# Unprocessed slots of all batches moved behind one branch at the end, in a state-space and mixture-of-experts kernel

## The chip, the cores and the metric

The kernel runs on one core of one Trainium2 chip. The metric is the device time of one execution in microseconds, as the median of several runs. An execution that is profiled gives in addition a trace of every engine: TensorE (PE), VectorE (DVE), ScalarE (ACT), GpSimd (POOL) and the DMA queues, which SyncE (SP) and POOL feed here.

## The reference

The inputs are x of 4 x 512 x 512 (batch, row, feature) and a context of 4 x 512 x 256, all fp32. Two blocks follow each other, each added to x behind a gate:

```python
x = x + tanh(g_xattn[0]) * ssm(ctx, layernorm(x), in_proj_w, conv_w, ...)   # a scan over 512 positions
x = x + tanh(g_ffn[0]) * moe(layernorm(x), W1, Wg, W2, Ws1, Wsg, Ws2, gate_w, gate_b, biases)
...
def step(state, xs):                      # 512 channels, 16 states each
    state = state * exp(d_t[..., None] * A) + (d_t * u_t)[..., None] * B_t[:, None, :]
    y_t = einsum('ben,bn->be', state, C_t)
...
output = expert(x, Ws1, Wsg, Ws2)         # shared: silu(x @ w1) * (x @ wg) @ w2, all 512 wide
for e in range(7):                        # each row goes to 3 of 7 experts
    output = output + expert(x, W1[e], Wg[e], W2[e]) * w_e[..., None]
```

## The kernel before, in words

The work of one batch has two halves. The first is the scan (`loop`, lines 549 to 725): 32 steps, each one state and 256 of the 512 channels. In a step POOL multiplies the rows B into the inputs (L637), ACT makes the decays `da` (L648), DVE scans (L679), multiplies by C (L595) and adds up (L602). The rows B and C come in groups of two states as `bc` (L324), one transfer of 1 MB on SP's queue for four steps. For batch 0 PE adds up instead of DVE (L609).

The second half is the mixture of experts. `post` turns y, adds it to x, normalizes (L756) and turns the result (`pn`, L764; copied by ACT at L767). `route` computes the logits (`pl` on PE, L820; `lg` on ACT, L822), ranks the experts on DVE, and gives each pair of row and expert a place, so that the rows of one expert stand together in tiles of 128 rows; POOL scatters the rows to their places in the DRAM tensor `xs` (L933, twelve indirect DMAs). `xs` exists twice, and batches take turns. The tensors are cleared at the start by `clear` (L208), three tiles a transfer.

The number of tiles depends on the data: with 512 x 3 pairs and 7 experts it is at most 18 (`n_slot`); 13 (`n_full`) are always processed. `experts` does so: the shared expert first (p1s, p2s, pos), then the tiles 0 to 12, each with its own expert's weights `w` (three transfers of 1 MB, addressed by a register that SP loads from the batch's `table`, L950 and L957), the gathered rows `xt` (L986), two products, their gating on DVE (L1155), a turn, a third product `po`, a scaling on ACT (L1015) and an indirect DMA that adds the rows to the output (L1020, POOL).

Tiles beyond the 13 are `rest` (L1027 to L1046): a branch on the count of tiles, `tc.If(n > i)` at L1029, whose body processes one tile and holds the branch for the next. The count is loaded into a register of all five engines at the last tile (L1215) and `rest` follows the last tile of each batch. At the end of an untaken branch each engine makes up for the semaphore counts of the body, and SP waits for the semaphores of its DMA queues.

The order of the work is written out by hand. Both halves are generators; `moe` runs post, route and experts, and between its pieces the scan of the next batch is moved on by as many steps as the table `STEPS` says (per batch: one digit for each piece of `post`, one for each of `experts`). `PIECES` does the same for what prepares the batch after that (`ahead`). Engines work their instructions off in this order.

Of the kernel before, what the change touches and what calls it, by code (L numbers as in the profile page):

```python
# [10 lines left out]
F32 = mybir.dt.float32  # L11
# [6 lines left out]
P = 128  # L18
# [3 lines left out]
NE = 7  # L22
# [13 lines left out]
STEPS = {  # L36
    0: ("000000", "101011010100110100110120111101110200010101111101101001"),
    1: ("100000", "201001001010110100110201201101110100101101201101100101"),
    2: ("000001", "201011010000110100110200011100200110101110200111000000"),
    3: ("000000", "000000000000000000000000000000000000000000000000000000"),  # L40
}

PIECES = {
    0: "000000002010112021101100222002011020220222010002201110",
    1: "000000101100111111111012112002022101122210211002100001",
    2: "",
# [5 lines left out]
def gated_ssm_moe(  # L52
# [29 lines left out]
    n_slot = lambda nt: (nt * P * TOPK + NE * (P - 1)) // P  # L82
    NSLOT = n_slot(NC)

    const = ctx.enter_context(tc.tile_pool(name="const", bufs=1))
# [56 lines left out]

    between = const.tile([P, 1], F32, tag="between", name="between")
    mhalf = const.tile([P, NC], F32, tag="mhalf", name="mhalf")
    nc.gpsimd.memset(mhalf, -0.5)
# [41 lines left out]

    xs = [store.tile([NSLOT * P, D + NW], F32, tag=f"xs{k}", name=f"xs{k}") for k in range(2)]

# [12 lines left out]
    def clear():  # L202

        nc.sync.dma_start(acc[(B - 1) * L : (B - 1) * L + P, :], empty[0][:, 0:D])
        for dst, src in zip(xs, empty):
            for i in range(0, NSLOT, 3):
                k = min(3, NSLOT - i)
                nc.sync.dma_start(  # L208
                    dst[i * P : (i + k) * P, :].rearrange("(i p) d -> p i d", p=P),
                    src.unsqueeze(1).to_broadcast([P, k, D + NW]),  # L210
                )
                yield
# [518 lines left out]

    held, routed = {}, {}

# [79 lines left out]
    def route(q):  # L813
# [98 lines left out]
        posk = tile_("posk", [nt, TOPK])  # L912
        nc.vector.tensor_reduce(posk, pk, AX.X, ALU.add)
        place = small.tile([P, nt, TOPK], I32, tag="place", name=f"place_{q}")
        nc.vector.tensor_copy(place, posk)
# [9 lines left out]
        nc.vector.tensor_reduce(expert, past, AX.X, ALU.add)  # L925
        table = small.tile([P, slots + 1], I32, tag="table", name=f"table_{q}")
        nc.vector.tensor_scalar(table[:, 0:slots], expert, NE - 1.0, None, ALU.min)
        nc.vector.tensor_copy(table[:, slots : slots + 1], upto[:, NE - 1 : NE])  # L928
        routed[q] = expert, table

        for t in range(nt):
            for k in range(TOPK):
                put = nc.gpsimd.indirect_dma_start(  # L933
                    xs[q % 2], bass.IndirectOffsetOnAxis(ap=place[:, t, k : k + 1], axis=0), xns[:, t, :], None
                )
# [48 lines left out]
    def rows_in(q, i):  # L984
        xt = two.tile([P, D + NW], F32, tag="xt", bufs=4, name=f"xt_{q}_{i}")[:, 0:D]
        nc.sync.dma_start(xt, xs[q % 2][ts(i, P), 0:D])  # L986
        return xt

    def slot_rows(q, expert):
# [4 lines left out]
        ex = small.tile([P, slots, NW], F32, tag="ex", name=f"ex_{q}")  # L994
        nc.sync.dma_start(ex, xs[q % 2][0 : slots * P, D : D + NW].rearrange("(i p) c -> p i c", p=P))
        yield
# [7 lines left out]
        nc.vector.tensor_tensor(of, of, ex[:, :, 0:NE], ALU.mult)  # L1004
        weight = small.tile([P, slots], F32, tag="weight", name=f"weight_{q}")
        nc.vector.tensor_reduce(weight, of, AX.X, ALU.add)
        nc.vector.scalar_tensor_tensor(weight, ex[:, :, NE], b * L - 0.5, weight, ALU.is_gt, ALU.mult)
        row = small.tile([P, slots], I32, tag="row", name=f"row_{q}")
        nc.vector.tensor_copy(row, ex[:, :, NE])
# [14 lines left out]

    slot_of = {}

    def rest(q, i, table, n, into):  # L1027
# [20 lines left out]
    def experts(q):  # L1048
# [144 lines left out]
        for i in range(last_tile + 1):  # L1193
# [19 lines left out]
            if i > 2:  # L1213
                W[i - 1].load(2)
            if i == last_tile:  # L1215
                n = nc.values_load(
                    table[0:1, slots : slots + 1], min_val=0, max_val=slots,
                    skip_runtime_bounds_check_because="no more tiles than slots can be in use",
                )
            yield  # L1220
# [33 lines left out]
            if i == last_tile:  # L1254
                W[i].load(2)

                into = [wpool.tile([P, NC, D], F32, tag=f"w{k}", name=f"w{k}_r{q}") for k in range(3)]
                if q + 1 < len(CHUNKS):
# [28 lines left out]
        else:  # L1287
            while adds:
                adds.pop(0)()
        rest(q, last_tile + 1, table, n, into)  # L1290

    def moe():
# [5 lines left out]
        for q, (b, _, _) in enumerate(CHUNKS):  # L1298
# [6 lines left out]
            for i, _ in enumerate(experts(q)):  # L1305
# [4 lines left out]
                if q + 1 < len(CHUNKS) and CHUNKS[q + 1][0] in loop_done:  # L1310
# [3 lines left out]
                    if more:  # L1314
                        yield q + 1, 0, next(at[q + 1])

    def first_loads():
# [75 lines left out]
```

## Time and profile before

| what | value |
| --- | --- |
| median of 3 runs | 1055.65 us (1055.58 to 1058.12) |
| the profiled execution | 1059.25 us |
| its span from first to last instruction | 1057.2 us |
| mean granted TensorE clock | 0.96 |
| batch 0's first logits to its last tile | 168 to 404 us |
| batch 1's | 412 to 642 us |
| batch 2's | 643 to 851 us |
| batch 3's | 852 to 1046 us |

The page of the profile gives busy times by engine, then the span in 40 slices (each digit a tenth), then what waited for what. An engine's idle time is named by what released it: "PE pn L764 <- PEq L1029" means that PE's instruction of line 764 stood behind an instruction of line 1029 in PE's own queue. Slices of PE, DVE, the granted clock and the DMA engines:

```profile
PE   9587867799999897999999888899999999999995
DVE  6999978999999997899999999888999531100000
PEclk9699888899999998999999999999999999999998
DMA  4197420499899965689899945889999449999974
```

### The profile page before, as it was taken

To read this page: it belongs to the slowest core of one execution; us is meant where nothing else is said; L and a number is where in the kernel's file an instruction comes from. 1 tells how busy PE (TensorE), PEld (TensorE's weight loads), DVE (VectorE), ACT (ScalarE), POOL (GpSimd) and SP (SyncE) were. 2 spreads that over 40 slices of the span, in tenths; PEclk is the share of its full clock that TensorE was granted. 3 is DMA by queue.
4 is the path that set the end of the run, shared out by engine and by line. 5 is a ranking of instruction groups with operands and counts; after the bars stand their busy time and mean duration, and the time that the engine had idled before them with its cause. 6 is when DMAs were issued, how large, how long until landed. Compare 5 with 4: busy or idle time off the path is not lost. (4 is left out here: it accounts for less than half of the span.)

```text
span 1057.2 us, 8951 instructions
## 1 busy us (share of the span) xinstructions
PE 952.6 (90%) x2540; PEld 430.9 (41%) x2540; DVE 798.7 (76%) x987; ACT 551.5 (52%) x770; POOL 497.4 (47%) x328
## 2 busy tenths in 40 slices
PE   9587867799999897999999888899999999999995
PEld 3232323344344443434344443344444444444442
DVE  6999978999999997899999999888999531100000
ACT  5857733547696664446797745536677220122221
POOL 2489942563564643653645546744565214011111
PEclk9699888899999998999999999999999999999998
DMA  4197420499899965689899945889999449999974
GB/s 141 53 345 262 160 80 0 157 332 331 282 355 318 324 186 188 214 322 353 298 331 295 369 122 192 290 281 336 375 376 362 133 146 341 345 318 322 340 233 83
DMA packets 138043, 272.11 MB, mean 257 GB/s; under 512 B 17134, under 2 KB 17134, under 8 KB 137982
## 3 DMA queue, kind: packets, MB, share of 16 engines
q1 hardware_dynamic: 126174, 244.19, 65.5%
q0 software_dynamic: 11328, 26.42, 10.8%
q10 hardware_dynamic: 480, 0.79, 0.2%
q8 instruction: 26, 0.43, 0.2%
q14 instruction: 35, 0.29, 0.1%
HBM read 230.65 MB, written 40.71 MB: 257 GB/s over the span
## 5 line engine op out<-in xcount | busy, mean ns | idle before, releaser
L637 POOL TENSOR_TENSOR h<-bc,home 128x1024 f32<-128x1024 f32 x128 | 309.2, 2422 | 238.6 <-DVE home L602 200.0
L981 PE MATMUL p<-w,turned_x 128*128 128x512 f32 x824 | 374.5, 598 | 12.4 <-ACT h L1238 4.7
L679 DVE TENSOR_TENSOR_SCAN h<-da,h 128x512 f32<-128x512 f32 x256 | 297.5, 1206 | 9.3 <-ACT da L648 6.8
L648 ACT ACTIVATE da<-home,a_neg 128x512 f32<-128x512 f32 x256 | 174.5, 689 | 226.6 <-DVE h L679 225.8
L981 PEld LDWEIGHTS p<-w,turned_x 128*128 128x128 f32 x824 | 152.7, 191 | 188.4 <-issue 168.7
L981 PE MATMUL po<-w,turned_h 128*128 128x512 f32 x408 | 185.4, 598 | 7.7 <-ACT yo L1015 5.1
L1020 POOL DMA_INDIRECT out_dram<-yo,row x52 | 95.9, 1845 | 189.0 <-ACT yo L1015 156.4
L595 DVE TENSOR_TENSOR h<-h,bc 128x1024 f32<-128x1024 f32 x96 | 135.8, 1415 | 1.0
L1155 DVE TENSOR_TENSOR h<-h,p 128x512 f32<-128x512 f32 x51 | 34.2, 671 | 120.0 <-PE p L981 120.0
L602 DVE TENSOR_TENSOR home<-home,h 128x1024 f32<-128x1024 f32 x96 | 119.6, 1246 | 3.1
L981 PEld LDWEIGHTS po<-w,turned_h 128*128 128x128 f32 x408 | 74.2, 192 | 84.6 <-issue 74.7
L609 PE MATMUL sum<-hc,ident 128*128 128x512 f32 x128 | 69.3, 684 | 21.7 <-POOL hc L595 12.1
L933 POOL DMA_INDIRECT xs<-xn,place x48 | 55.6, 1159 | 44.7 <-DVE table L928 25.1
L648 ACT ACT_TABLE_LOAD x53 | 68.0, 1283 | 1.3 <-ACT xd L318 0.4
L973 ACT COPY turned_x<-pt_x 128x512 f32<-128x512 f32 x52 | 30.2, 581 | 67.3 <-PE pt_x L968 67.2
L1015 ACT ACTIVATE yo<-po,weight 128x512 f32<-128x512 f32 x52 | 35.5, 683 | 55.1 <-PE po L981 49.7
L1114 PE MATMUL pos<-w_s,home 128*128 128x512 f32 x128 | 58.4, 610 | 4.0 <-DVE home L1078 2.3
L981 PE MATMUL p1s<-home,w_s 128*128 128x512 f32 x128 | 59.1, 599 | 1.7 <-ACT sgs L1075 1.7
L981 PE MATMUL p2s<-home,w_s 128*128 128x512 f32 x128 | 60.0, 612 | 0.0
L973 ACT COPY turned_h<-pt_h 128x512 f32<-128x512 f32 x51 | 29.5, 578 | 44.2 <-PE pt_h L968 44.2
L609 PEld LDWEIGHTS sum<-hc,ident 128*128 128x128 f32 x128 | 25.6, 212 | 63.4 <-issue 25.7
L1238 ACT ACT_TABLE_LOAD x38 | 48.8, 1283 | 0.5
(160 smaller groups left out, 848.0 us busy)
## 6 DMA issues: line engine op xcount, KB each, us to landing
w<-in_w_dram SPq DMA_DIRECT2D x104, 1024.0 KB, 8.3
w<-in_wg_dram SPq DMA_DIRECT2D x52, 1024.0 KB, 10.8
bc<-rows SPq DMA_DIRECT2D x32, 1024.0 KB, 6.6
xt<-xs SPq DMA_DIRECT2D x52, 256.0 KB, 6.5
xs<-empty SPq DMA_DIRECT2D x12, 780.0 KB, 11.0
w_s<-in_ws_dram SPq DMA_DIRECT2D x8, 1024.0 KB, 9.3
xx<-in_x_dram SPq DMA_DIRECT2D x4, 1024.0 KB, 7.4
w_s<-in_wsg_dram SPq DMA_DIRECT2D x4, 1024.0 KB, 11.4
```

The source lines that it names most:

```text
L595: engine.tensor_tensor(hc, h, c_k.unsqueeze(1).to_broadcast([P, W, L]), ALU.mult)
L602: nc.vector.tensor_tensor(y[:, c0 : c0 + W, :], y[:, c0 : c0 + W, :], h, ALU.add)
L609: nc.tensor.matmul(sums[c1 + w], ident, hc1[:, w, :], start=False, stop=(k1 == NS - 1))
L637: nc.gpsimd.tensor_tensor(h, b_k.unsqueeze(1).to_broadcast([P, W, L]), layer.u[:, c0 : c0 + W, :], ALU.mult)
L648: nc.scalar.activation(da, layer.delta[:, c, :], AF.Exp, scale=a_neg[:, c, k : k + 1])
L679: nc.vector.tensor_tensor_scan(h[:, w, :], da, h[:, w, :], 0.0, ALU.mult, ALU.add)
L933: put = nc.gpsimd.indirect_dma_start(xs[q % 2], bass.IndirectOffsetOnAxis(ap=place[:, t, k : k + 1], axis=0), xns[:, t, :], None)
L973: nc.scalar.copy(t, pt)
L981: nc.tensor.matmul(p[:, 0:n], lhs(c), rhs(c), start=(c == 0), stop=(c == NC - 1))
L1020: nc.gpsimd.indirect_dma_start(acc, bass.IndirectOffsetOnAxis(ap=slot_of[q][1][:, i : i + 1], axis=0), yo, None, compute_op=ALU.add,)
L1114: nc.tensor.matmul(pos[t], hTs[:, c, ts(t, P)], ws.t[2][:, c, :], start=(c == 0), stop=(c == NC - 1))
L1238: nc.scalar.activation(hs[i], p1.pop(i), AF.Silu)
```

## The change

- The call of `rest` at the end of each batch goes, and with it the load of the count at the last tile. A new function `rests`, called once after the last batch, loads the largest count of the four batches (`most`) and holds all four batches' `rest` chains, each with its own count, behind one branch.
- So that the rows beyond 13 tiles outlive their batch, `xs` becomes one tensor: two halves of 13 tiles that batches take turns in, and four stretches of 5 tiles, one for each batch. `clear` fills 46 tiles instead of 36, in 17 transfers instead of 12. Places of 13 x 128 and over are moved by an offset: two more small DVE operations in `route`, and one that keeps the largest count. The weights' rows `ex` come in two transfers instead of one. `table`, `weight` and `row` are kept for all four batches.
- The digits of `STEPS` and `PIECES` are other ones.

```diff
 STEPS = {
-    0: ("000000", "101011010100110100110120111101110200010101111101101001"),
-    1: ("100000", "201001001010110100110201201101110100101101201101100101"),
-    2: ("000001", "201011010000110100110200011100200110101110200111000000"),
+    0: ("000000", "101011010100110100110120111101110200000201102101101000"),
+    1: ("100100", "021001001001101100110201201101110100101101201101100101"),
+    2: ("000001", "110011010020000200101101101101110110110002011101000000"),
...
 PIECES = {
-    0: "000000002010112021101100222002011020220222010002201110",
-    1: "000000101100111111111012112002022101122210211002100001",
+    0: "000000002010111121101100222002011002122210211010120011",
+    1: "000000101100110211021021202002021220222120011102000001",
...
-    xs = [store.tile([NSLOT * P, D + NW], F32, tag=f"xs{k}", name=f"xs{k}") for k in range(2)]
+    xs = store.tile([(2 * NF + B * NR) * P, D + NW], F32, tag="xs", name="xs")
+    first_place = lambda q: q % 2 * NF * P
+    rest_place = lambda q: (2 * NF + q * NR) * P
+    tile_place = lambda q, i: first_place(q) + i * P if i < NF else rest_place(q) + (i - NF) * P
...
-        for dst, src in zip(xs, empty):
-            for i in range(0, NSLOT, 3):
-                k = min(3, NSLOT - i)
+        parts = [(first_place(k), NF, empty[k]) for k in range(2)]
+        parts += [(rest_place(0), (B - 1) * NR, empty[0]), (rest_place(B - 1), NR, empty[1])]
+        for at, n, src in parts:
+            for i in range(0, n, 3):
+                k = min(3, n - i)
...
+        beyond = tile_("beyond", [nt, TOPK])
+        nc.vector.tensor_scalar(
+            beyond, posk, NF * P - 0.5, float(rest_place(q) - NF * P - first_place(q)), ALU.is_gt, ALU.mult
+        )
+        nc.vector.scalar_tensor_tensor(posk, posk, float(first_place(q)), beyond, ALU.add, ALU.add)
...
+        if q == 0:
+            nc.vector.tensor_copy(most, upto[:, NE - 1 : NE])
+        else:
+            nc.vector.tensor_tensor(most, most, upto[:, NE - 1 : NE], ALU.max)
...
+    def rests():
+        slots = n_slot(NC)
+        number = small.tile([P, 1], I32, tag="number", name="number")
+        nc.vector.tensor_copy(number, most)
...
+        n = count_of(number[0:1, 0:1])
+        into = [wpool.tile([P, NC, D], F32, tag=f"w{k}", name=f"w{k}_r") for k in range(3)]
+        with tc.If(n > NF):
+            for q in range(len(CHUNKS)):
+                rest(q, NF, tables[q], count_of(tables[q][0:1, slots : slots + 1]), into)
...
-            if i == last_tile:
-                n = nc.values_load(
-                    table[0:1, slots : slots + 1], min_val=0, max_val=slots,
-                    skip_runtime_bounds_check_because="no more tiles than slots can be in use",
-                )
...
-        rest(q, last_tile + 1, table, n, into)
...
+        rests()
```

More of the change, by code (lines that the diff above doesn't have):

```diff
@@ L83, in gated_ssm_moe @@
     NSLOT = n_slot(NC)
+    NF = n_full(NC)
+    NR = NSLOT - NF
     const = ctx.enter_context(tc.tile_pool(name="const", bufs=1))
@@ L143, in gated_ssm_moe @@
     between = const.tile([P, 1], F32, tag="between", name="between")
+    most = const.tile([P, 1], F32, tag="most", name="most")
     mhalf = const.tile([P, NC], F32, tag="mhalf", name="mhalf")
@@ L204, in clear @@
         nc.sync.dma_start(acc[(B - 1) * L : (B - 1) * L + P, :], empty[0][:, 0:D])
-        for dst, src in zip(xs, empty):
-            for i in range(0, NSLOT, 3):
-                k = min(3, NSLOT - i)
+        parts = [(first_place(k), NF, empty[k]) for k in range(2)]
[3 more added lines that the diff above has]
+                k = min(3, n - i)
                 nc.sync.dma_start(
-                    dst[i * P : (i + k) * P, :].rearrange("(i p) d -> p i d", p=P),
+                    xs[at + i * P : at + (i + k) * P, :].rearrange("(i p) d -> p i d", p=P),
                     src.unsqueeze(1).to_broadcast([P, k, D + NW]),
@@ L729, in ssm @@
             yield from loop(b, sums if b == 0 else None)
-    held, routed = {}, {}
+    held, routed, tables = {}, {}, {}
     def post(q):
@@ L925, in route @@
         nc.vector.tensor_reduce(expert, past, AX.X, ALU.add)
-        table = small.tile([P, slots + 1], I32, tag="table", name=f"table_{q}")
+        table = small.tile([P, slots + 1], I32, tag="table", bufs=B, name=f"table_{q}")
         nc.vector.tensor_scalar(table[:, 0:slots], expert, NE - 1.0, None, ALU.min)
@@ L929, in route @@
         routed[q] = expert, table
+        tables[q] = table
+        if q == 0:
+            nc.vector.tensor_copy(most, upto[:, NE - 1 : NE])
+        else:
+            nc.vector.tensor_tensor(most, most, upto[:, NE - 1 : NE], ALU.max)
         for t in range(nt):
@@ L933, in route @@
                 put = nc.gpsimd.indirect_dma_start(
-                    xs[q % 2], bass.IndirectOffsetOnAxis(ap=place[:, t, k : k + 1], axis=0), xns[:, t, :], None
+                    xs, bass.IndirectOffsetOnAxis(ap=place[:, t, k : k + 1], axis=0), xns[:, t, :], None
                 )
@@ L985, in rows_in @@
         xt = two.tile([P, D + NW], F32, tag="xt", bufs=4, name=f"xt_{q}_{i}")[:, 0:D]
-        nc.sync.dma_start(xt, xs[q % 2][ts(i, P), 0:D])
+        nc.sync.dma_start(xt, xs[tile_place(q, i) : tile_place(q, i) + P, 0:D])
         return xt
@@ L994, in slot_rows @@
         ex = small.tile([P, slots, NW], F32, tag="ex", name=f"ex_{q}")
-        nc.sync.dma_start(ex, xs[q % 2][0 : slots * P, D : D + NW].rearrange("(i p) c -> p i c", p=P))
+        for i, n in ((0, NF), (NF, NR)):
+            at = tile_place(q, i)
+            nc.sync.dma_start(ex[:, i : i + n, :], xs[at : at + n * P, D : D + NW].rearrange("(i p) c -> p i c", p=P))
         yield
@@ L1004, in slot_rows @@
         nc.vector.tensor_tensor(of, of, ex[:, :, 0:NE], ALU.mult)
-        weight = small.tile([P, slots], F32, tag="weight", name=f"weight_{q}")
+        weight = small.tile([P, slots], F32, tag="weight", bufs=B, name=f"weight_{q}")
         nc.vector.tensor_reduce(weight, of, AX.X, ALU.add)
         nc.vector.scalar_tensor_tensor(weight, ex[:, :, NE], b * L - 0.5, weight, ALU.is_gt, ALU.mult)
-        row = small.tile([P, slots], I32, tag="row", name=f"row_{q}")
+        row = small.tile([P, slots], I32, tag="row", bufs=B, name=f"row_{q}")
         nc.vector.tensor_copy(row, ex[:, :, NE])
@@ L1025, in gated_ssm_moe, with count_of @@
     slot_of = {}
+    def rests():
+        slots = n_slot(NC)
+        number = small.tile([P, 1], I32, tag="number", name="number")
+        nc.vector.tensor_copy(number, most)
+        def count_of(ap):
+            return nc.values_load(
+                ap, min_val=0, max_val=slots,
+                skip_runtime_bounds_check_because="no more tiles than slots can be in use",
+            )
+        n = count_of(number[0:1, 0:1])
[3 more added lines that the diff above has]
+                rest(q, NF, tables[q], count_of(tables[q][0:1, slots : slots + 1]), into)
     def rest(q, i, table, n, into):
@@ L1255, in experts @@
                 W[i].load(2)
-                into = [wpool.tile([P, NC, D], F32, tag=f"w{k}", name=f"w{k}_r{q}") for k in range(3)]
                 if q + 1 < len(CHUNKS):
```

## The prediction, made before the result was known

> **What bounds the kernel now.** I read the page's busy list and slices first, then the busy time by stage, then the branch's line, then the timeline around it, and last the chain that ended last.
>
> ```profile
> span 1057.2 us, 8951 instructions
> PE 952.6 (90%) x2540; PEld 430.9 (41%) x2540; DVE 798.7 (76%) x987; ACT 551.5 (52%) x770; POOL 497.4 (47%) x328
> ...
> xt<-xs SPq DMA_DIRECT2D x52, 256.0 KB, 6.5
> ```
>
> PE is busy for 90%, but no engine bounds all stages. 52 gathered tiles are read, 4 batches of 13, so with these inputs no batch has a 14th tile: the branch is never taken, before or after. All that is at stake is what an untaken branch, its place and the order cost. Busy time by stage (columns: PE, PEld, DVE, ACT, POOL, granted clock, DMA):
>
> ```profile
> 225.00:400.00 175.00, 167.29 (x465) 76.79 (x463) 172.56 (x186) 117.40 (x162) 88.72 (x41) 0.98 0.90 301
> 400.00:460.00 60.00, 53.38 (x135) 22.88 (x135) 50.76 (x80) 27.11 (x36) 36.89 (x35) 0.94 0.64 212
> 460.00:640.00 180.00, 168.26 (x480) 78.18 (x479) 176.17 (x194) 122.47 (x169) 88.47 (x43) 0.99 0.89 300
> 640.00:700.00 60.00, 51.72 (x123) 21.22 (x122) 50.04 (x78) 27.80 (x35) 39.76 (x35) 0.97 0.69 225
> 700.00:850.00 150.00, 148.03 (x441) 71.70 (x440) 129.15 (x136) 89.58 (x121) 71.69 (x35) 1.00 0.93 317
> 850.00:1034.00 184.00, 182.45 (x505) 84.73 (x504) 22.44 (x64) 35.07 (x58) 31.66 (x36) 1.00 0.88 289
> ```
>
> During the tiles of batches 0 and 1 (225 to 400, 460 to 640) DVE, which runs the scan of the next batch, is busy for 98.6 and 97.9%: it sets the pace. From about 700 on PE does (98.7%, then 99.2%). Between them lie two passages of 60 us, each the start of a batch, in which neither is full: PE lacks 6.6 and 8.3 us, DVE 9.2 and 10.0. A gain must come from there, from 850, or from the tail. Now the branch's own line, and who waited for it:
>
> ```profile
> L1029 SPq EVENT_SEMAPHORE  x36: 17/17/17, 400.5 to 1039.9; - x36
> L1029 SPq COMPARE_BRANCH  x4: 45/48/50, 400.0 to 1034.0; - x4
> ...
> L1029 PEldq COMPARE_BRANCH  x4: 424/1680/6429, 400.8 to 1042.9; - x4
> L1029 ACTq COMPARE_BRANCH  x4: 45/45/45, 404.5 to 1046.0; - x4
> ...
> L1029 POOLq COMPARE_BRANCH  x4: 53/53/53, 405.0 to 1046.7; - x4
> ...
>   PE pn L764: 3.1, 1
>   PE pl L820: 0.9, 1
> ```
>
> The branch stands four times, once a batch. It takes 45 to 72 ns on every engine but PE, where it takes up to 6.4 us. The timeline from 407 shows what followed the 6.4 us one:
>
> ```profile
> 407.51 2.50 PE L764 MATMUL pn<-ident,xn 128*128 128x128 f32 x16 [3.06 <-PEq L1029]
> ...
> 411.62 5.54 PE L820 MATMUL pl<-home,gw 128*7 128x512 f32 x8 [1.61 <-ACT home L767]
> ...
> 417.19 0.68 ACT L822 ACTIVATE lg<-pl,gb 7x512 f32<-7x512 f32 x1 [5.62 <-PE pl L820]
> 417.77 1.28 ACT L648 ACTIVATE da<-home,a_neg 128x512 f32<-128x512 f32 x2
> 418.54 2.34 DVE L679 TENSOR_TENSOR_SCAN h<-da,h 128x512 f32<-128x512 f32 x2 [4.64 <-ACT da L648]
> ```
>
> Read downwards: PE stood 3.06 us; its next eight pl matmuls took 5.54 us, where the same eight at 852 took 3.60 (the stage's granted clock is 0.94); the logits on ACT waited for them; the decays (da) queued behind the logits; and DVE, the pace-maker, stood 4.64 us.
>
> **The change part by part.** The profiled execution took 1059.25 us, 1057.2 of span and 2.05 around it; it lies 3.6 above the median of 1055.65. I sum differences inside the profile and take them from the median.
>
> *Three of four branches go.* Batch 0's (404): PE loses 3.06 of idling and 5.54 - 3.60 = 1.94 at the low clock, 5.0 in all, and DVE 4.64. As DVE sets the pace afterwards, I take DVE's: **-4.6**. With the branch gone the turned rows (pn) start 3.06 earlier and the logits about 5.0 earlier, more than the 4.64 that DVE waited; late next is the wait of pl for ACT's copies (1.61 before), which has DVE work beside it. Batch 1's (636 to 646): PE waits 1.6 there, but for ACT's copies, queued behind da's that wait for DVE: 0, at best -1.6. There SP stands from 636.7 to 646.0 behind its semaphores, holding one bc load back; its reader is a scan group (4 steps of about 4.9 us) later and no POOL or DVE wait names it: 0. Batch 2's (847 to 852): PE sets the pace and waits 0.9 for the branch on ACT: **-0.9**. The count's register loads at each last tile (0.27 to 0.55 us, by the queues) have no wait behind them: 0.
>
> *Added on DVE, per batch:* two operations of 128x12 for the place, and one of 128x1 for the largest count. Nearest rows: place (CAST 128x12, 173 ns), L907 (190 ns), off (161 ns), about 0.22 from start to start: 0.6 a batch. In batches 0 and 1 DVE has no cover: **+1.2**. In batches 2 and 3 PE sets the pace; what is queued behind is the twelve scatters on POOL, then SP's reads of xt (issued at 892.5, read by PE at 897.9 without a gap). Cover is the shared products; without it 0.6 each. I take 0.
>
> *DMAs.* Clearing takes 17 transfers instead of 12 and 10 tiles, 2.6 MB, more, in loop 0 between 57 and 98, and about one scan group longer. SP's queue also carries the bc loads: +0 to +1.7, the one DVE gap in that passage (82.4 to 84.1). The stage after it has DMA at 0.38, and the first scatter is at 197: I take 0. The weights' rows (ex) come in two transfers, 0.47 us of SP's queue each time, with a weight load behind it that is used two tiles later: 0. One tensor for both halves of xs makes scatters wait for reads of the batch before, which end some 40 us earlier: 0.
>
> *The branch that stays.* Now the count is copied on DVE and loaded by five engines at the very end, and the jump passes 20 tiles' code instead of 5. The chain of the tail is this:
>
> ```profile
> 1033.59 0.70 ACT yo L1015
> ...
> 1040.92 5.28 DMA out_dram<-yo,row
> ...
> 1046.73 0.05 POOLq L1029
> ...
> 1046.96 1.54 POOL out_dram L1020
> ```
>
> After it POOL runs a DRAIN of 7.3 us (1048.65 to 1055.96), which no other engine comes near. PE's copy of the jump may take 2.9 as it does here or 6.4 and still ends by 1052.5: covered. POOL's is not. Queued behind its branch are its semaphores, the DRAIN and the closing barrier, for which all wait. Price: the register load, 0.30, and the jump. From below 0.05 (its own row, over 5 tiles' code), from above 2.9 (PE's row at this place); the DRAIN may hide it (its start would move, its end need not). POOL's code per tile is far shorter than PE's, but four times as much is passed: between, 1.2. Together **+1.5**, ends 0 and +3.2.
>
> [...]
>
> *Tables.* The counts hardly change (29 to 34 steps a batch's row); some 20 entries move a step by one or two places. What they can win: PE's 8.3 us in 640 to 700, where waits for DVE and ACT (2.3, 1.7, 1.1, 0.9) are what early steps of batch 2 put ahead, and the new row has one step fewer before the first products. What they can lose: one step placed ahead of what PE waits for, 1.23 + 1.23 + 2 x 1.21 = 4.9. Ends -8.3 and +4.9; I take a quarter of the room, **-2.1**, nearest to the 2.3 of the longest of these waits.
>
> Sum: -4.6 - 0.9 + 1.2 + 1.5 - 2.1 = -4.9. Forecast 1055.65 - 4.9 = **1050.7 us**.
>
> **Rivals.**
> *Nothing reaches the end* (0.24). DVE fills the 4.64 gap, but as pace-maker waits as much at the next place where it needs PE (its other waits in 400 to 460 are 2.5 and 0.8), and the tables give nothing. Left: -0.9 + 1.2 + 1.5, with a third of the 4.64, -1.5: about 0, **1055.9**. For: PE's stall at 365 cost DVE nothing. Against: after 460 DVE has no idle time in which a gain could be lost.
> *The tables pay more* (0.07). Half of the 8.3 goes: -4.6 - 0.9 + 1.2 + 0.3 - 4.2 = -8.2, **1047.5**.
> *A new wait in place of the old* (0.09), slower. Batch 1's first row becomes 100100: a scan step now stands ahead of the second pair's normalization. If PE has no tile left to do there, pn and the logits come 4.9 later and the clock falls (1.9): with the 4.6 won, +2.2. With the jump at its upper end: 2.2 - 0.9 + 1.2 + 3.2 = +5.7, **1061.4**. It decides when PE's gap ahead of pn exceeds the 3.06 of now. Against it: that step comes off the two that stand behind the logits now, so DVE does not lose it.
>
> **How the numbers follow.** The likeliest case has 0.60, its own range 1048 to 1052.4. A measurement here can tell 0.3%, 3.2 us, from no change. Faster: 0.60 + 0.07 = 0.67; same: 0.24; slower: 0.09. The range of 1045.5 to 1057 takes in the first three nearly whole and leaves out the slower case and the far ends.
>
> **What would show it.** Right: no PE wait for a branch before 1000; pl of batch 1 at about 3.6 us, clock near 0.98 in that stage; DVE's wait for da there under 1; the whole shifted by 4 to 5 us from then on; pl of batch 3 without the 0.9; PE's idle time in batch 2's first 60 us down by about 2. Wrong: POOL's DRAIN starting over 3 us after the last scatter's issue and as long as now; a DVE gap of over 3 us at any of the three joins; a PE wait for pn in batch 1 of 3 us or more.

## The result, and the profile after

The changed kernel takes **1050.73 us** (median of 11 runs, 1049.66 to 1052.54) where the kernel before takes 1055.58 in the same comparison (11 runs, 1052.95 to 1062.54). The ratio is 0.9953, with a 95% interval of 0.9937 to 0.9969: about 5.0 us less, at least 3.3 and at most 6.7. The forecast was 1050.7. Its total was right; some of its terms were right and others were off in ways that offset each other, and the runs below take them apart.

The page's span and busy lines, and those 14 of the 17 transfers clearing `xs` that move three tiles:

```profile
span 1050.7 us, 8879 instructions
PE 949.1 (90%) x2540; PEld 430.6 (41%) x2540; DVE 791.7 (75%) x1000; ACT 545.6 (52%) x765; POOL 496.5 (47%) x328
...
xs<-empty SPq DMA_DIRECT2D x14, 780.0 KB, 9.9
```

PE does the same 2540 matmuls, and DVE has 13 instructions more: three in each of four batches and the copy of the count. In this kernel lines stand lower on the page than before: the turned rows `pn` are at L774 (before L764), the logits `pl` at L830 (L820), the decays `da` at L658 (L648), the scan at L689 (L679), the output scaling `yo` at L1038 (L1015), the add at L1043 (L1020). The end branch is at L1064, the closing barrier at L1423 (L1389).

Busy time by stage, columns as before (PE, PEld, DVE, ACT, POOL, granted clock, DMA, GB/s):

```profile
400.00:460.00 60.00, 55.43 (x148) 24.11 (x147) 55.65 (x88) 26.64 (x37) 38.37 (x36) 1.00 0.68 227
460.00:640.00 180.00, 168.18 (x477) 76.88 (x476) 176.09 (x193) 122.76 (x171) 90.09 (x43) 0.99 0.88 305
640.00:700.00 60.00, 55.99 (x137) 24.46 (x137) 51.74 (x82) 29.14 (x36) 40.66 (x35) 0.97 0.72 226
700.00:850.00 150.00, 146.24 (x436) 69.68 (x435) 116.45 (x133) 84.71 (x117) 67.00 (x34) 1.00 0.92 317
```

In 400 to 460, where the first branch stood, DVE's busy time rose by 4.9 (50.76 to 55.65) and the clock from 0.94 to 1.00; the stage after is as full as it was. The timeline there, without the stall:

```profile
402.26 1.04 PE L774 MATMUL pn<-ident,xn 128*128 128x128 f32 x8
...
404.18 1.17 PE L774 MATMUL pn<-ident,xn 128*128 128x128 f32 x8 [0.88 <-DVE xn L766]
...
406.97 3.60 PE L830 MATMUL pl<-home,gw 128*7 128x512 f32 x8 [1.61 <-ACT home L777]
...
410.61 0.68 ACT L832 ACTIVATE lg<-pl,gb 7x512 f32<-7x512 f32 x1 [3.69 <-PE pl L830]
411.19 1.28 ACT L658 ACTIVATE da<-home,a_neg 128x512 f32<-128x512 f32 x2
...
411.96 2.34 DVE L689 TENSOR_TENSOR_SCAN h<-da,h 128x512 f32<-128x512 f32 x2 [0.21 <-ACT da L658]
```

Now `pn` runs in two halves as its rows come, PE's wait ahead of it is 0.88 instead of 3.06, `pl` takes 3.60 instead of 5.54, and DVE waits 0.21 for `da` instead of 4.64. This is the first term of the forecast, line for line.

At batch 2's old branch, however, the wait is still there. PE's waits from 838 to 850:

```profile
PE pl L830 <- ACT yo L1038: 0.8, 1, 0.8
```

`pl` of batch 3 waited 0.9 for ACT's branch; it waits 0.8 now for ACT's scaling of the last output, the instruction that stood in front of that branch.

And the tail has grown. The rows of the end branch on POOL, then those of the load of the count and of the closing barrier (minimum, median and longest in ns, first and last start):

```profile
L1064 POOLq EVENT_SEMAPHORE  x5: 17/43/1654, 1041.0 to 1043.0; - x5
...
L1064 PEldq COMPARE_BRANCH  x1: 3542/3542/3542, 1035.0 to 1035.0; - x1
...
L1064 POOLq COMPARE_BRANCH  x1: 53/53/53, 1038.3 to 1038.3; - x1
L1064 POOLq INC_SWDGE_SEM  x1: 1468/1468/1468, 1043.1 to 1043.1; - x1
```

```profile
L1057 POOLq TENSOR_LOAD <-number x1: 501/501/501, 1037.7 to 1037.7; - x1
```

```profile
L1423 POOLq DRAIN  x3: 46/107/5295, 1044.6 to 1050.4; - x3
```

And the closing barrier's of the kernel before:

```profile
L1389 POOLq DRAIN  x3: 51/165/7315, 1048.6 to 1056.9; - x3
```

POOL's branch begins at 1038.3 and lists 53 ns, but its next instruction starts at 1041.0: 2.8 us in between, taken here as the jump. Then one semaphore wait of the join (the semaphore instructions at the branch's end, five on POOL) takes 1.65; it ends at 1042.87, and the last add's own transfer lands at 1042.84. `INC_SWDGE_SEM` takes 1.47, and the DRAIN starts at 1044.6, 6.6 after the last add was issued (1037.94). It then takes 5.3 instead of 7.3. From the last add to the end of the span 12.8 us pass, 10.2 before.

Where the time went, by the starts of the same work in both profiled executions (after minus before, us):

```
batch 0's logits                -0.46     batch 2's logits            -7.16
batch 0's first tile            -0.10     batch 2's first tile       -10.12
batch 0's ninth tile            +1.71     batch 2's fifth tile        -9.05
batch 0's thirteenth tile       -2.86     batch 3's logits            -9.01
batch 1's logits, first         -4.64     last add                    -9.01
batch 1's logits, last ended    -6.58     end of the span             -6.45
```

The shift comes at two places, batch 1's start and batch 2's start, keeps its size through the tiles between, and 2.6 of it is lost in the tail. The two profiled executions lie 3.6 and 1.8 above their medians, so these shifts are larger than the medians' 5.0.

Starts on PE vary from execution to execution: in run 1 below, whose order of work is the same up to there, batch 0's logits start 3.4 earlier than before. DVE, which sets the pace in this part, varies far less. From its 65th scan instruction (the first of batch 1, at 175.12 before) to its 145th (457.30) every kernel has the same DVE work but for the added operations. The time between the two starts, from the traces of the kernels and of the runs below:

| kernel | us |
| --- | --- |
| before | 282.2 |
| the changed kernel; runs 5, 6 and 7, which equal it up to here | 275.4; 275.5, 275.4, 275.5 |
| run 1, tables alone | 279.9 |
| run 2, order alone | 276.6 |
| run 3, only the last branch | 277.5 |
| run 4, short bodies | 280.9 |
| run 8, small operations six times | 282.0 |
| run 9, new tables, only the last branch | 275.4 |
| runs 10 and 11, fewer small operations | 276.0, 275.9 |

### The profile page after: what moved, and what is told of

Same layout as the page of the kernel before. It is cut to its first block, busy times and chain, and to the rows that moved or that the text cites. A ratio compares the mean times of both kernels' runs of the same rounds, so it can differ in the third digit from the quotient of the medians.

```text
span 1050.7 us, 8879 instructions
## 1 busy us (share of the span) xinstructions
PE 949.1 (90%) x2540; PEld 430.6 (41%) x2540; DVE 791.7 (75%) x1000; ACT 545.6 (52%) x765; POOL 496.5 (47%) x328
## 4 chain that ended last, share of the span: by engine, by line
PE 39%; DVE 35%; issue 8%; POOL 6%; ACT 6%; DMA 5%; SPq 0%; DVEq 0%; POOLq 0%; ACTq 0%
PE p L1002 18%; DVE h L689 13%; PE po L1002 9%; DVE h L605 6%; POOL h L647 4%; PE pos L1155 3%; DVE home L293 2%; PE p1s L1002 2%; PE p2s L1002 2%; POOL hc L605 2%; DVE home L612 2%; DMA cT<-in_ctxT_dram 2%; DVE h L1196 1%; DMA bc<-rows 1%; PE pt_h L989 1%
## 5 line engine op out<-in xcount | busy, mean ns | idle before, releaser
L1002 PE MATMUL p<-w,turned_x 128*128 128x512 f32 x824 | 373.3, 597 | 12.5 <-ACT h L1274 4.6
L689 DVE TENSOR_TENSOR_SCAN h<-da,h 128x512 f32<-128x512 f32 x256 | 297.4, 1205 | 7.7 <-POOL h L647 4.7
L658 ACT ACTIVATE da<-home,a_neg 128x512 f32<-128x512 f32 x256 | 174.5, 689 | 216.7 <-DVE h L689 216.0
L1043 POOL DMA_INDIRECT out_dram<-yo,row x52 | 95.1, 1830 | 188.1 <-ACT yo L1038 171.1
L605 DVE TENSOR_TENSOR h<-h,bc 128x1024 f32<-128x1024 f32 x96 | 127.0, 1323 | 0.9
L1038 ACT ACTIVATE yo<-po,weight 128x512 f32<-128x512 f32 x52 | 35.5, 684 | 59.0 <-PE po L1002 53.2
```

The source lines that it names most:

```text
L605: engine.tensor_tensor(hc, h, c_k.unsqueeze(1).to_broadcast([P, W, L]), ALU.mult)
L658: nc.scalar.activation(da, layer.delta[:, c, :], AF.Exp, scale=a_neg[:, c, k : k + 1])
L689: nc.vector.tensor_tensor_scan(h[:, w, :], da, h[:, w, :], 0.0, ALU.mult, ALU.add)
L1002: nc.tensor.matmul(p[:, 0:n], lhs(c), rhs(c), start=(c == 0), stop=(c == NC - 1))
L1043: nc.gpsimd.indirect_dma_start(acc, bass.IndirectOffsetOnAxis(ap=slot_of[q][1][:, i : i + 1], axis=0), yo, None, compute_op=ALU.add,)
```

## Experiments

Each was timed in five rounds against the kernel before. Single runs of one kernel spread over several us, so ratios carry intervals of about 2 us on either side; a change "of so many us" below is the ratio's distance from 1 times 1055.65. The time of before in the three groups of runs was 1055.74 (the first four), 1055.00 (the next four) and 1056.67 (the last three). Line numbers are each kernel's own.

**1. The tables alone**: before, with the new STEPS and PIECES.

```diff
-    0: ("000000", "101011010100110100110120111101110200010101111101101001"),
+    0: ("000000", "101011010100110100110120111101110200000201102101101000"),
...
```

> The kernel before with the new STEPS and PIECES, its four branches where they were. Theory (the first branch's stall on PE made most of the gain, the tables about 2 us in the first 60 us of batch 2 and 2 us in batch 0's last tiles): PE still stands about 3 us at batch 0's branch, and about 1052 to 1054 us come out. Rival (the tables made the gain): 1048 to 1051 us, since the tail then lacks the later branch's price.

1053.22 us (1050.77 to 1056.32), ratio 0.9975 [0.9955, 0.9995]: -2.6 us. The branches and their waits stayed:

```profile
L1029 PEldq COMPARE_BRANCH  x4: 424/1752/6269, 395.2 to 1036.8; - x4
...
  PE pn L764: 3.0, 1
```

The tables are worth something by themselves, about what the forecast took. On DVE they take 2.3 off (282.2 to 279.9), in batch 0's last tiles. 2.0 of it are two multiplications by C (L595, at 343.86 and 354.93 before) that ran beside POOL's multiplication by B (L637) and took 2.2 us each; with the new tables each takes 1.2. The first of them, before and then in this run:

```profile
342.06 2.94 POOL L637 TENSOR_TENSOR h<-bc,home 128x1024 f32<-128x1024 f32 x1
343.86 2.23 DVE L595 TENSOR_TENSOR h<-h,bc 128x1024 f32<-128x1024 f32 x1
```

```profile
337.78 2.35 POOL L637 TENSOR_TENSOR h<-bc,home 128x1024 f32<-128x1024 f32 x1 [0.43 <-DVE home L602]
340.45 1.22 DVE L595 TENSOR_TENSOR h<-h,bc 128x1024 f32<-128x1024 f32 x1
```

**2. The order alone**: the changed kernel with the old STEPS and PIECES.

```diff
-    0: ("000000", "101011010100110100110120111101110200000201102101101000"),
+    0: ("000000", "101011010100110100110120111101110200010101111101101001"),
...
```

> The kernel after with the old STEPS and PIECES. Theory: batch 0's stall is gone (4.7 us), the tail's 2.6 us are paid, so 1052 to 1054 us, with DVE's gap ahead of batch 1's logits gone. Rival (the tables made the gain): 1056 to 1059 us, the old time and the dearer tail.

1053.58 us (1051.05 to 1056.8), ratio 0.9985 [0.9965, 1.0005]: -1.6 us. `pl` of batch 1 takes 3.60 here too and the tail 12.5. Order and tables (-1.6 and -2.6) add up to the whole (-5.0) within their intervals; nothing shows that the one needs the other.

**3. Only the last branch**: before, without the count load and the branch after batches 0, 1 and 2. It leaves out what those batches would have beyond their thirteenth tile (nothing with these inputs).

```diff
-            if i == last_tile:
+            if i == last_tile and q + 1 == len(CHUNKS):
                 n = nc.values_load(
...
-        rest(q, last_tile + 1, table, n, into)
+        if q + 1 == len(CHUNKS):
+            rest(q, last_tile + 1, table, n, into)
```

> The kernel before with the branch and the count's load left out after batches 0, 1 and 2 (their tiles beyond the 13th are left out, and there are none with these inputs); old tables, old places, old clearing. Theory: batch 0's 4.7 us go and nothing else, about 1051 us; batch 2's wait of 0.9 us for the output's scaling stays. Rival one (the tables made the gain): 1055 to 1056. Rival two (the forecast's sum, with batch 2's 0.9 paid by the branch): 1050.

1051.04 us (1048.37 to 1054.55), ratio 0.9947 [0.9925, 0.9969]: -5.6 us. On DVE 4.7 of it appear from the 65th to the 145th scan (282.2 to 277.5), all at batch 0's branch: up to the 133rd scan the two profiles agree within 0.1. So the three branches carry as much as the whole change brings. Yet PE's waits from 838 to 850 show that batch 2's branch was not what `pl` waited for:

```profile
PE pl L820 <- ACT yo L1015: 0.8, 1, 0.8
PE po L981 <- ACT turned_h L973: 0.4, 1, 0.4
```

**4. Short bodies**: before, with bodies of one tile instead of five, the branches where they were. It leaves out the tiles beyond the fourteenth. The jump passes a fifth of the code; the join after it stays.

```diff
             add_rows(q, i, out_scaled(q, i, po, yo))
-            if i + 1 < n_slot(CHUNKS[q][2]):
-                rest(q, i + 1, table, n, into)
```

> The kernel before with branches whose body is one tile instead of five (the tiles beyond the 14th are left out, and there are none): joins, loads and waits stay, only the jump is shorter. Theory (the jump past 5 tiles of PE's code was the cost): PE's branch takes 0.5 us or less at all four places, the stall of 3.06 us goes, 1051 to 1052 us. Rival (the join, with SP's and POOL's waits for their transfers, was the cost): the stall stays, 1055 to 1056 us.

1053.76 us (1050.36 to 1057.27), ratio 0.9974 [0.9953, 0.9995]: -2.7 us, half of what leaving the branch out gave. First the branch's rows, then the timeline behind it:

```profile
L1029 PEldq COMPARE_BRANCH  x4: 223/320/358, 402.6 to 1042.1; - x4
```

```profile
407.11 1.97 PE L764 MATMUL pn<-ident,xn 128*128 128x128 f32 x16 [0.87 <-ACTq L1029]
...
411.25 5.30 PE L820 MATMUL pl<-home,gw 128*7 128x512 f32 x8 [2.17 <-ACT home L767]
...
417.93 2.34 DVE L679 TENSOR_TENSOR_SCAN h<-da,h 128x512 f32<-128x512 f32 x2 [2.57 <-ACT da L648]
```

PE's branch is down from 6.4 to at most 0.36 us, so the long time was the jump over the body. But all sixteen `pn` still start together, behind the join (their wait names ACT's branch); `pl` still takes 5.30 us where it takes 3.60 in the changed kernel; DVE still waits 2.57. What PE meets there is ACT: `pn` starts at 407.11, just behind ACT's scaling of the last output (406.32 to 407.01); without the branch (run 3) it starts at 404.55, ahead of that scaling. Both theories had half: by the medians some 2.7 of the gain is the jump, the remaining 2.9 the meeting of the engines at the branch with a body of one tile. DVE's wait divides alike: 2.1 of 4.64 went, 2.57 stayed. (Over the whole stretch to the 145th scan DVE is only 1.2 shorter, as in this profile it waits 0.8 for PE at 396, ahead of the branch.) By the medians the split is uncertain by some 3 us either way; that both halves exist is shown by the profile.

**5. No end branch**: the changed kernel without `rests()`, so all tiles beyond the thirteenth are left out.

```diff
-        rests()
```

> The kernel after with the branch at the end and its count's load left out (all tiles beyond the 13th are left out, and there are none). It prices the tail. Theory (the late branch costs 2.6 us: POOL's join waits for the last addition's transfer before the closing DRAIN can start): 1047.5 to 1048.5 us, with 9 to 10 us from the last addition's issue to the end of the span instead of 12.8. Rival (DRAIN and barrier take as long in any case): 1050 to 1051.

1048.33 us (1048.0 to 1052.56), ratio 0.9932 [0.9911, 0.9953]: -7.2 us, 2.2 below the changed kernel. The tail is 9.9 instead of 12.8:

```profile
L1422 POOLq DRAIN  x3: 51/169/8952, 1040.7 to 1050.6; - x3
```

The DRAIN starts at 1040.7, beside the last add's issue, and takes 8.95. It ends 8.7 after that add's issue (1040.96), as it ends 9.0 after it in the kernel before (1046.95 to 1055.96), but 11.9 in the changed one. In these traces the DRAIN hides a branch when it starts 1.7 us after the add's issue (before), and no longer when it starts 6.6 after (the changed kernel).

**6. The branch ahead of the last add**: `rests()` is called before the last tile's add.

```diff
         else:
+            rests()
             while adds:
...
-        rests()
```

> The kernel after with the branch put ahead of the last indirect addition, behind its scaling on ACT, so that nothing of it stands between that addition and the DRAIN. Theory: POOL's count, jump (2.8 us) and join lie between the last two additions, where POOL waits anyway, and 2 to 2.7 us of the tail come back: about 1048 us. Rival (POOL's jump is on the path wherever it stands): the last addition is issued 2 to 4 us later and 1050 to 1052 come out.

1050.09 us (1049.34 to 1050.98), ratio 0.9946 [0.9926, 0.9967]: -5.7, 0.7 below the changed kernel, which the intervals don't separate. The tail from the last add is 9.6 again, but the add itself waits:

```profile
L1064 POOLq EVENT_SEMAPHORE  x5: 17/43/43, 1035.8 to 1036.1; - x5
L1064 POOLq COMPARE_BRANCH  x1: 53/53/53, 1032.2 to 1032.2; - x1
```

POOL's branch starts at 1032.2, the next instruction at 1035.8 (a jump of 3.6), the join lasts to 1037.7, and the add is issued at 1038.72, about 2 later than without. Moved, the price is paid in part in the other place.

**7. One batch in the end branch**: the changed kernel whose end branch holds batch 3's chain alone. It leaves out what batches 0 to 2 would have beyond their thirteenth tile.

```diff
-            for q in range(len(CHUNKS)):
+            for q in range(len(CHUNKS) - 1, len(CHUNKS)):
```

> The kernel after with only the last batch's chain behind the branch at the end (the other batches' tiles beyond the 13th are left out, and there are none): place and count's load as after, the body a quarter. Theory (the body of 20 additions counts up all of POOL's DMA semaphores, so that the join has to wait for the last addition; one of 5 does not): tail as before, 1048 to 1048.5 us. Rival (the late load and place cost, not the body): 1050 to 1051.

1048.79 us (1046.33 to 1050.98), ratio 0.9934 [0.9911, 0.9957]: -7.0, and a tail of 9.7.

```profile
L1064 POOLq EVENT_SEMAPHORE  x3: 17/43/43, 1038.4 to 1038.6; - x3
L1064 POOLq COMPARE_BRANCH  x1: 53/53/53, 1038.0 to 1038.0; - x1
L1064 POOLq INC_SWDGE_SEM  x1: 1478/1478/1478, 1038.7 to 1038.7; - x1
```

From the branch to the next instruction 0.5 us pass instead of 2.8, and no semaphore wait of the join exceeds 43 ns, where one took 1654. With 5 adds in the body the join has three semaphore instructions instead of the five that it has with 20, and none waits for the add just issued. So the tail's price is the size of the body, in two ways: POOL's jump, and the join.

**8. The small operations six times**: the changed kernel with fifteen more small DVE operations in each batch's routing, five times the three that the change adds, of the same shapes.

```diff
+        again = tile_("again", [nt, TOPK])
+        for _ in range(5):
+            nc.vector.tensor_scalar(again, posk, NF * P - 0.5, 1.0, ALU.is_gt, ALU.mult)
+            nc.vector.scalar_tensor_tensor(again, posk, 1.0, again, ALU.add, ALU.add)
+            nc.vector.tensor_tensor(again[:, 0, 0:1], upto[:, 0:1], upto[:, NE - 1 : NE], ALU.max)
```

> The kernel after with the three added small operations of the route on DVE done five times more, into a scratch tile: 15 operations, about 15 x 0.22 = 3.3 us of DVE's time a batch. By the forecast's reckoning (batches 0 and 1 have no cover) 6.6 us more, 1057 us. Rival (DVE's pace has slack there, as the trace of the changed kernel shows no loss at that place): 0 to 2 us more, 1051 to 1053 us.

1062.22 us (1060.95 to 1064.79), ratio 1.0064 [1.0042, 1.0086]: 11.5 above the changed kernel by medians, more than either expectation. In its profile the four batches give 3.7 (it is 0.6 late already at batch 0's logits), 2.9, 2.8 and 0.7. Batch 2 is not covered, then; batch 3 is. What waits is POOL's first scatter. The waits of 165 to 235, in the changed kernel and then in this one:

```profile
POOL xs L954 <- DVE table L942: 8.6, 1, 8.6
```

```profile
POOL xs L959 <- DVE table L947: 11.6, 1, 11.6
...
PE p1s L1007 <- ACT sgs L1121: 2.7, 1, 2.7
```

The scatter waits 3.0 us more for fifteen operations, 0.2 for each, the forecast's price of one; behind it PE waits 2.7 for ACT. A fifth of the whole 11.5 would be 2.3 us.

**9. New tables, only the last branch**: the third run with the new STEPS and PIECES; it leaves out the same (what lies beyond the thirteenth tile, not the ninth as the expectation has it). It has nothing of what the change adds (no operations, places, longer clearing or divided `ex`), and the end branch of before.

```diff
-            if i == last_tile:
+            if i == last_tile and q + 1 == len(CHUNKS):
...
```

> The kernel before with the new STEPS and PIECES and without the count load and branch after batches 0, 1 and 2, so that only batch 3's is left (it leaves out what would go beyond the ninth tile in the first three batches, which is empty on this input). It has none of the added VectorE operations, places, clearing or ex DMAs of the change. Its neighbour is the changed kernel with one batch in its end branch (1048.8 us), which has them all. Theory 'the added operations cost 2 us' (a fifth of the fifteen operations' price): 1046 to 1047.2, some 2 us below that neighbour, the difference already there at the first expert tiles of batches 1 and 2. Rival 'they cost what the forecast took, half a microsecond for each of batches 0 and 1': 1047.4 to 1048. Rival 'they cost nothing at five small operations a batch, the price of fifteen starts where a slack is used up': 1048.5 to 1049.2. If the tables and the order add, the sum of the two runs alone (-4.7 and -2.5 from before) says 1048.0 to 1048.5 with before near 1055.4.

1049.36 us (1045.28 to 1050.97), ratio 0.9926 [0.9902, 0.9949]: -7.8 us; branches and tables apart were -5.6 and -2.6. Its neighbour with all the added parts (run 7) has -7.0. The median lies just above the range of the rival that takes them at nothing, but before was 1.7 higher in this group than in run 7's; by the ratios the price is 0.8, with anything from -2.6 to 4.2 inside the intervals. The medians don't decide. DVE's time up to the 145th scan does for batches 0 and 1: 275.4 here and 275.5 in run 7, so there the added parts cost nothing in the end. Run 10 shows why.

**10. Fewer small operations**: one added operation a batch instead of three. The sum writes the integer places itself, and the maximum is taken once, from the tables, in batch 3's last tile.

```diff
-        nc.vector.scalar_tensor_tensor(posk, posk, float(first_place(q)), beyond, ALU.add, ALU.add)
...
-        nc.vector.tensor_copy(place, posk)
+        nc.vector.scalar_tensor_tensor(place, posk, float(first_place(q)), beyond, ALU.add, ALU.add)
...
-            nc.vector.tensor_tensor(most, most, upto[:, NE - 1 : NE], ALU.max)
...
+                nc.vector.tensor_tensor(number, last(0), last(1), ALU.max)
+                for k in range(2, len(CHUNKS)):
+                    nc.vector.tensor_tensor(number, number, last(k), ALU.max)
```

> The changed kernel with one added VectorE operation for each batch in place of three to four: the addition of the first place writes the integer places itself, and the maximum of the tiles in use is taken once, from the tables of all batches, in batch 3's last tile, so the count is ready before the last branch. Theory 'each small operation ahead of the scatter costs its time, 0.2 us': two of three gone in batches 0, 1 and 2, -1.0 to -1.5 us, and -0.2 in the tail: 1049.0 to 1049.6 where after gives 1050.7. Rival 'they cost nothing': 1050.3 to 1050.9.

1052.41 us (1050.58 to 1054.26), ratio 0.9967 [0.995, 0.9984]: -3.5 us. That is 1.5 less gain than the changed kernel has, where 1.0 to 1.5 more was expected; the intervals of the two overlap. POOL's wait for `table` in batch 0 is 8.4 instead of 8.6, so the operations did go, but nothing came of it.

The traces show where it went. On DVE the added operations do cost about 0.2 us each at first: from the 65th to the 73rd scan (batch 0's routing) 31.5 us pass without them, 32.0 with three and 31.7 with one; from the 137th to the 141st (batch 1's) 16.8, 17.4 and 17.0. The third one, however, the largest count, stands between `table`, for which POOL's first scatter waits, and DVE's next multiplication by C. With it the multiplication and the scatter of batch 1 start together, and the scatter takes 1.00 us; without it the multiplication is 0.07 ahead, and the scatter takes 2.02. In the changed kernel, then in this run:

```profile
427.96 1.27 DVE L605 TENSOR_TENSOR h<-h,bc 128x1024 f32<-128x1024 f32 x1
427.97 1.00 POOL L954 DMA_INDIRECT xs<-xn,place  x1 [6.80 <-issue]
```

```profile
427.08 1.22 DVE L604 TENSOR_TENSOR h<-h,bc 128x1024 f32<-128x1024 f32 x1
427.15 2.02 POOL L947 DMA_INDIRECT xs<-xn,place  x1 [6.59 <-issue]
```

So with the third operation all that follows on POOL comes 1.0 earlier, its multiplication by B too, beside which DVE's next multiplication by C stands:

```profile
434.12 2.96 POOL L647 TENSOR_TENSOR h<-bc,home 128x1024 f32<-128x1024 f32 x1
436.06 2.12 DVE L605 TENSOR_TENSOR h<-h,bc 128x1024 f32<-128x1024 f32 x1
```

```profile
434.32 2.97 POOL L646 TENSOR_TENSOR h<-bc,home 128x1024 f32<-128x1024 f32 x1
435.07 3.30 DVE L604 TENSOR_TENSOR h<-h,bc 128x1024 f32<-128x1024 f32 x1
```

DVE ends 1.1 us after POOL in both, though it began 1.0 earlier here. In the six kernels with the third operation (the changed one, runs 2, 5, 6, 7 and 8) the scatter takes 1.0 and this multiplication 2.1 us; in the seven without it, 2.0 and 3.3. So 1.2 come back in batch 1. At batch 2's start the same happens (but for run 5): the multiplication there takes 1.23 in the changed kernel and 2.13 in this run. What DVE makes for PE (`home`) comes later by that, PE waits 2.3 instead of 1.4, and the 26 matmuls behind that wait take longer. On PE, in the changed kernel, in this run and in run 7:

```profile
672.84 1.13 PE L1155 MATMUL pos<-w_s,home 128*128 128x512 f32 x2 [1.39 <-DVE home L1119]
674.89 13.12 PE L1155 MATMUL pos<-w_s,home 128*128 128x512 f32 x26 [0.93 <-ACT sgs L1116]
```

```profile
673.27 1.39 PE L1148 MATMUL pos<-w_s,home 128*128 128x512 f32 x2 [2.30 <-DVE home L1112]
675.33 14.14 PE L1148 MATMUL pos<-w_s,home 128*128 128x512 f32 x26 [0.67 <-ACT sgs L1109]
```

```profile
672.40 1.13 PE L1155 MATMUL pos<-w_s,home 128*128 128x512 f32 x2 [1.41 <-DVE home L1119]
674.46 11.43 PE L1155 MATMUL pos<-w_s,home 128*128 128x512 f32 x26 [0.93 <-ACT sgs L1116]
```

The same 26 matmuls take 13.12, 14.14 and 11.43 us; the granted clock from 675 to 688 is 0.87, 0.78 and 1.00. The first and the last had the same waits ahead of them, to 0.02 us, and still differ by 1.7.

**11. Fewer operations and the branch ahead of the last add**: runs 10 and 6 together, a candidate that leaves no work out.

```diff
         else:
+            rests()
             while adds:
...
```

> As the run with fewer small operations, and the end branch stands before the last add instead of after it. Candidate for a version better than both kernels that leaves no work out. With -1.0 to -1.5 from the operations and -0.6 to -1 from the place of the branch: 1048.3 to 1049.2; the tail from the last add to the end 9.6 instead of 12.5 us, the last add 2 us later. If the operations cost nothing: 1049.7 to 1050.2. If the earlier count lets POOL's branch come earlier and its jump overlap ACT's last scaling, the last add is delayed by less than 2 us and the time falls under 1048.3.

1051.15 us (1049.26 to 1054.63), ratio 0.9947 [0.9928, 0.9967]: -5.6 us. Against run 10 the branch's place gives about 2 (tail 9.8 instead of 12.9, the last add 1.5 later), against the changed kernel 0.6, inside the intervals. No version that does all of the work is shown to beat the changed kernel.

## Why the prediction came out right, point by point

- **Batch 0's branch, -4.6: right in size and place, half right in its cause.** The three branches are worth -5.6 [-7.9, -3.3] (run 3). At this place DVE gains 4.7 with the old tables (run 3 against before) and 4.5 with the new ones (run 9 against run 1). The forecast laid it all to PE's 6.4 us jump and the low clock after it (0.65 from 411.6 to 417.2 before, 1.00 from 406.9 to 410.6 after). Run 4 shows that the jump is about half; the rest is the join, at which PE waits 0.87 for ACT, so that all `pn` start together and late even with a branch of 0.3 us. The rival that nothing reaches the end is refuted: the shift keeps its size through the tiles of batch 1, where DVE sets the pace (busy 176.1 of 180 us from 460 to 640).
- **Batch 1's branch, 0: right.** PE's wait ahead of batch 2's logits is 1.6 for ACT's copies before, in run 3 and in the changed kernel; from the end of batch 1's logits to the end of batch 2's, run 3 is 0.2 shorter than before and the changed kernel 0.6. On DVE, from the 145th to the 201st scan, 0.8 are gained with the old tables (182.0 before, 181.2 in run 3) and nothing with the new ones (182.0 in run 1, 181.9 in run 9).
- **Batch 2's branch, -0.9: wrong.** The step that failed is that the wait named after the branch would go with it. It was ACT's last output scaling that PE waited for, before and after (0.8 against 0.9); the branch was only the last thing that ACT did before the release.
- **Added DVE operations, +1.2: right as their price, but a gain of the same size was left out.** They cost DVE 0.5 in batch 0 and 0.6 in batch 1 (run 10), 0.2 each, as forecast. The step that failed is that nothing else would come of them: in batch 1 the third one lets POOL's first scatter take 1.0 us instead of 2.0, and DVE's multiplication beside POOL's is 1.2 shorter by that. So the changed kernel and run 9, which lacks the operations, both need 275.4 us to the 145th scan, and run 10, which takes the third one away too, gained nothing. That batch 2 has cover is refuted for fifteen more (run 8, 2.8 there). The remainder of the sum of medians, -5.0 less the terms -5.6, -2.6 and +2.2, is +1.0, for these and all else that the change adds, with an uncertainty of several us, so it may be nothing.
- **Clearing and `ex`, 0**: DVE's 61st scan, behind the clearing (57 to 108), starts at 140.68 where it started at 140.51 before, and DVE's longest waits from 40 to 225 have the same names and nearly the same sizes (5.1 for PE's sums where it was 5.4, 2.5 for POOL, 1.7 for `da`). No price is seen. The size taken for `ex` was wrong all the same: the second transfer holds SP's queue for 5.6 to 6.5 us in each batch, not 0.47. Before, the weight load behind the single transfer took 3.9 to 6.6 instead, so little changed for what follows.
- **End branch, +1.5: +2.2 by run 5, inside its ends, but only one of two mechanisms was named.** The jump on POOL was taken at 1.2 and measured 2.8. The join's wait until the last add's own landing (1.65) wasn't in the sum: with 20 adds in the body the join has five semaphore instructions on POOL, with 5 it has three, none over 43 ns (run 7). Of what both delayed, the shorter DRAIN (5.3 instead of 7.3) gave 2.0 back. POOL's jump was 2.8 us over 20 tiles' code and 0.5 over 5 (run 7); why it takes that long is not shown.
- **Tables, -2.1: -2.6 [-4.8, -0.5] by run 1, right in size by luck.** A quarter of the room was a guess between far ends, set near PE's wait of 2.3 for DVE in 640 to 700. That wait doesn't go with the tables: it is 2.3 with the new ones in runs 1 and 9, and 1.4 with the old ones in run 2. In twelve of the thirteen traces (run 8 has no such wait) it is 2.3 where DVE's multiplication at batch 2's start takes 2.1, and 1.4 where it takes 1.2 (run 10). What the tables gain lies in batch 0's last tiles: 2.3 on DVE in run 1, 2.1 in run 9 against run 3, nearly all of it two multiplications by C that no longer meet POOL's. With the added operations there (run 2 against the changed kernel) it is 1.2.

The sum of measured terms: branches -5.6, tables -2.6, end branch +2.2, remainder +1.0, in all -5.0; forecast -5.5, -2.1, +1.5, +1.2, in all -4.9. The agreement to 0.1 us is luck, as intervals of 2 us on each term show; what is borne out is the sign and the order of size of each group, and the rival with a new wait ahead of `pn` is refuted (0.88 us of wait, not 3 or more). The tables' gain arose in another place than the forecast looked, and the added operations' cost was given back by an effect that it didn't have.

## What to carry to other kernels

In this kernel an untaken branch cost its jump (6.4 us on PE at batch 0) and what its join waits for (DVE still lost 2.57 with a branch of 0.3). Take it out of the places where the pace-making engine depends on an engine that has to meet the others, and keep the one that stays short enough that the closing DRAIN still hides it (here the tail took 9.7 us with 5 tiles in the body, 12.8 with 20). A wait that the profile puts down to a branch may belong to the instruction ahead of it; look at whether the same tile's release comes any earlier without the branch. Change the length of a body and its presence separately, since leaving the branch out removes jump and join at once. A small operation added on the pace-making engine, 0.2 us each here, gave back more than its time in one place (1.2 in batch 1) and cost more in another (11.5 for fifteen a batch, by the medians), by what then starts beside another engine's work: follow the starts of the same instructions in both traces, which here show fractions of a microsecond that the medians don't.

## What the runs showed of the hardware that was not expected

- **A jump's time lies outside the branch's own row on POOL.** The row says 53 ns each time; the next instruction starts 0.2 to 0.5 us later over 1 or 5 tiles' code (before, runs 1, 3, 4 and 7) and 2.6 to 3.6 over 20 (the changed kernel, runs 2, 6 and 11). On PE the time is in the row, but the length alone doesn't set it: at most 0.36 over 1 tile, but 6.4, 0.45, 0.42 and 2.9 over the same 5 tiles in the four batches of the kernel before, 3.9 over 5 in run 7 and 3.5 over 20 in the changed kernel. The shortest is 0.22 (run 4). Why batch 0's takes 6.4 and the next two 0.4 stays open.
- **The DRAIN on POOL at the end** takes 5.3 to 9.0 us in five kernels, and there is the shorter the later it starts after the last add's issue: 9.0 beside it (runs 5 and 6), 7.3 when 1.7 after (before), 6.3 when 2.6 after (run 7), 5.3 when 6.6 after (the changed kernel). In all but the changed kernel it ended 8.7 to 9.0 after that issue, in the changed one 11.9.
- **DVE and POOL slow each other down.** In the traces of both kernels from 165 to 860 DVE's multiplication by C takes 1.2 to 1.3 us where POOL idles or does anything but its multiplication by B, and more, up to 4.0 (before, at 452.13), only where that runs beside it. POOL's takes 2.3 to 2.4 in most places and 2.9 to 3.0 in most of those where the two overlap by 1.0 or more, but 2.36 beside that longest one. The first scatter of batches 0 to 2 takes 2.0 to 2.1 us where it starts 0.09 to 0.21 behind that multiplication by C (before, and batch 0 of the changed kernel; 0.07 in run 10), and 1.0 where both start within 0.02 (batches 1 and 2 of the changed kernel; 2.1 all the same once, in run 5).
- **Short idling of PE is sometimes followed by a slow stretch.** After waits of 1.4 and 0.9 us the same 26 matmuls took 11.4 us in one run (run 7) and 13.1 in another (the changed kernel), at a granted clock of 1.00 and 0.87 from 675 to 688; after 2.3 and 0.7 they took 14.1 at 0.78 (run 10). What sets the clock apart after the same waits is not shown. Whether it is part of why single runs of one kernel spread over several us was not tried.
